# A selective scan and a spectral filter: the input load, the root of the group norms and the loads of B and C at other slots

## The chip, the core and the metric

The kernel runs on one core of a Trainium2 chip. A core has five engines with an instruction queue each: PE (TensorE, matrix products and transposes), DVE (VectorE), ACT (ScalarE), POOL (GpSimd) and SP (SyncE, which here only issues DMAs). Each queue runs in program order; engines wait for one another, and for DMAs, by semaphores. The metric is the time of one execution on the device in microseconds (us), the median of several runs. A profile is one further execution, recorded by the hardware.

## The reference

The input x is (4, 128, 128, 128): batch, channel, height, width. Two layers follow.

Layer 0 is a selective scan over the 16,384 pixels of an image, channels 128, inner width 256, 16 states:

```
xm  = relu(x @ w1 + b1) @ w2 + b2
u,z = split(xm @ in_proj);   u = silu(causal_conv4(u))
dt,B,C = split(u @ x_proj)            # 8, 16 and 16 columns
delta  = softplus(dt @ dt_proj + b)
h = h * exp(delta * A) + delta * B * u      # per inner channel and state
y = (sum over states of h * C + u * D) * silu(z)
out = silu(group_norm(y @ out_proj, 4 groups)) + x
```

Layer 1 aggregates its input (group norm, a 128 by 128 product, relu, mean over the image, softmax over 4 weights), and filters each image in the frequency domain: forward transform, product with a mix of four complex filters and with the transform itself, backward transform, plus half of the input.

## The kernel before

**Tiling.** `block0` does layer 0 and the aggregation, `block1` the spectral filter. In `block0` an image is cut into 32 chunks of T = 512 pixels, so there are 128 chunks for four images. The 256 inner channels are 2 halves (j) of 128; each half is 4 groups (r) of 32 channels, and 32 channels with 4 states fill the 128 partitions. One such tile of 128 x 512 is scanned by one DVE instruction, `nc.vector.tensor_tensor_scan` (L405). A chunk has 2 x 4 x 4 = 32 of them, two a slot, so a chunk has NP = 16 slots.

**Order.** Nothing is scheduled by a tool: each piece of work is entered as (slot, phase, function) in `todo`, and L493 to L497 emit them slot by slot, in a slot by phase: turn, sums, pe, exps, late, act, pool, dbu, gate, scans, dve, end. The slots in `pre(k)` (L313) are relative to the chunk before k: slot 16 is the first slot in which chunk k is scanned. Negative slots lie in the chunk before that. So each engine, SP too, works on chunks k and k+1 interleaved. What this order does to one engine's queue is all that decides what may run when.

**The preparation of chunk k** (`pre`): `load` brings the chunk's input xt (one buffer) by SP; `h1_mm`, `h1_act`, `xm_mm`, `xm_act` are the first two products; `cv_mm`, `silu_act` make u; `xd_mm`, `xd_act` make dt, B and C as xd (40 x 512) and store B and C into a DRAM tile bc; `dt_mm`, `dt_act` make delta, and SP stores it into a DRAM tile dd, half by half; `du_pool` (L303, POOL) makes du = delta * u and SP stores it into dd too. The DRAM tiles are there to be read back spread over partitions:

- `bc_load` (L253): B as rB (four DMAs of 192 KB) and C as rC (four of 256 KB), each row copied to 32 partitions;
- `rep_load(j)` (L311): for half j, delta as rdelta and du as rdu (four DMAs of 256 KB each), each row copied to the 4 states of its channel. Half 0 is issued at slot 9, half 1 at slot 16. Both tiles have two buffers.

`du_turn` (PE) and `bt_act` (ACT) make the product delta * B * u for the first of every four tiles in another way, by way of transposes.

**The scan of a chunk.** ACT makes da = exp(delta * A) (`exps`, L387), POOL makes hb = rdu * rB for the other three of every four tiles (`dbu`, L354, at every even slot, two slots ahead of its scans), DVE scans (L405), then h is multiplied by rC, by DVE for two of four tiles (L407) and by POOL for the other two (`scans`, L412). PE sums over states (`sums`, L426). The first `dbu` of chunk k is emitted at slot 14 of the chunk before: it is the first instruction that reads rB of k and rdu of half 0 of k.

**SP's queue** in chunk k-1, in order: rep_load(1) of k-1 (slot 0), the store of bc (slot 4), the store of an output, bc_load (slot 5), two stores of delta (slot 6), xt of the next chunk (slot 7), two stores of du (slot 7, phase pool), rep_load(0) (slot 9). A DMA whose semaphore is not there holds up all that stand behind it.

**Norms.** `finish` applies the group norm of a finished image, its silu and the residual, while the next image is scanned; it reads the parts of x and of the output back (xr, of) in slots 13 and 14, in chunks 2 to 17 of the next image (48 chunks in all, called norm chunks below; the others are called plain), and then aggregates. `group_norm` (L500) is run twice an image: statistics on DVE, two small products with ACT work between them, then `root_act` (L529, a square root on ACT) and `invert` (L532, a reciprocal on DVE), and last what needs the result (`then`: three small ACT instructions, or the scaled weights of the aggregation, followed by `bias_mm` on PE and `bias_act` on ACT). The norms of the last image lie in `block1`, whose slots are thirds of a unit of eight channels of an image.

Of the kernel before, what the change touches and what calls it, by code (L numbers as in the profile page):

```python
# [146 lines left out]
def block0(tc, s):  # L147
# [4 lines left out]
    with ExitStack() as ctx:  # L152
# [22 lines left out]
        def pre(k):  # L175
# [130 lines left out]
            def rep_load(j):  # L306
# [4 lines left out]
                        nc.sync.dma_start(out=t[m * DG : (m + 1) * DG], in_=rows)  # L311

            return [  # L313
                (-9, "pe", load), (-7, "pe", h1_mm), (-6, "act", h1_act), (-5, "pe", xm_mm), (-4, "act", xm_act),
                (0, "pe", partial(cv_mm, 0)), (1, "pe", partial(cv_mm, 1)), (2, "act", silu_act),
                (NP - 3, "pe", z_mm), (NP - 1, "act", z_act), (NP + 2, "act", z_silu), (3, "pe", xd_mm), (4, "act", xd_act), (5, "pe", dt_mm), (5, "pe", xd_turn),
                (5, "act", bc_load), (6, "act", dt_act), (7, "act", xd_turn_act), (7, "pool", partial(du_pool, 0)),
                (7, "pool", partial(du_pool, 1)), (8, "pe", partial(du_turn, 0)), (9, "act", partial(rep_load, 0)),
                (8, "pool", partial(bt_act, 0, 0, 1)), (9, "act", partial(bt_act, 0, 1, 5)),
                (10, "act", partial(bt_act, 0, 5, 8)), (11, "pe", partial(du_turn, 1)),  # L320
                (11, "pool", partial(bt_act, 1, 0, 1)), (12, "act", partial(bt_act, 1, 1, 2)),
# [139 lines left out]
        todo = defaultdict(list)  # L461
        for k in range(n_chunks):
            for at, phase, f in pre(k) + post(k):
                todo[at + (k - 1) * NP, phase].append(f)
# [16 lines left out]
        for b in range(B - 1):  # L481
            for at, phase, f in finish(s, io, b, NP + 7, norm, agg):
                todo[at + (b + 1) * NCH * NP, phase].append(f)
# [16 lines left out]
def group_norm(s, io, b, mat, which, stat, at, then):  # L500


    nc = s.nc
    g = {}

    def small(n, m=1):
        g[n] = io.small.tile([P, m], F32, tag=n, name=f"{n}_{which}_{b}")
        return g[n]

    def aggregate():  # L510
        nc.vector.bn_aggr(small("mv", 2), stat().rearrange("p n q -> p (n q)"))

    def mean_mm():
        ps = g["ps"] = io.psum(f"gm_{which}_{b}")
        nc.tensor.matmul(ps[:, 0:1], getattr(s, mat), g["mv"][:, 0:1], start=True, stop=True)

    def spread_act():
        mv = g["mv"]
        nc.scalar.copy(small("mean"), g["ps"][:, 0:1])
        q = small("q")  # L520
        nc.scalar.activation(q, mv[:, 0:1], AF.Square, scale=-1.0, bias=g["mean"])
        nc.scalar.activation(q, q, AF.Identity, bias=mv[:, 1:2])

    def var_mm():
        ps = g["ps"] = io.psum(f"gv_{which}_{b}")
        nc.tensor.matmul(ps[:, 0:1], getattr(s, mat), g["q"], start=True, stop=True)

    def root_act():
        nc.scalar.activation(small("rstd"), g["ps"][:, 0:1], AF.Sqrt, bias=s.eps)  # L529

    def invert():
        nc.vector.reciprocal(g["rstd"], g["rstd"])  # L532
        then(g["mean"], g["rstd"])

    return [
        (at, "dve", aggregate), (at, "end", mean_mm), (at + 1, "act", spread_act), (at + 3, "pe", var_mm),
        (at + 3, "act", root_act), (at + 3, "dve", invert),
    ]


def finish(s, io, b, first, norm, agg, add="dve"):
# [87 lines left out]
    def weights_act():  # L629
        nc.scalar.activation(s.wts[b], g["lg"], AF.Identity, scale=g["total"])  # L630

    todo = group_norm(s, io, b, "g0", 0, lambda: stats[b], first, start)
    for i in range(NCH):
        at = norm(i)
# [3 lines left out]
        ]  # L638
    c = at[2] + 5
    todo += group_norm(s, io, b, "g1", 1, lambda: g["stat"], c, middle)  # L640
    todo += [(c + 4, "pe", bias_mm), (c + 4, "act", bias_act)]
    for i in range(NCH):
        at = agg(i)
        todo += [
# [3 lines left out]
    c = at[2] + 1  # L648
# [6 lines left out]
def block1(tc, s):  # L655
# [10 lines left out]
    with ExitStack() as ctx:  # L666
# [35 lines left out]
        t1 = norm(NCH - 1)[2] + 14  # L702
        todo = defaultdict(list)
        steps = finish(s, io, B - 1, 0, norm, lambda i: (t1 + i - 3, t1 + i, t1 + i, None), "add")
        for at, phase, f in steps:
            todo[at, phase].append(f)
# [269 lines left out]
```

## Time and profile before

| What | Value |
|---|---|
| median of 3 runs | 7330.66 us (7328.43 to 7332.73) |
| the profiled execution's own time | 7341.55 us |
| its span | 7339.5 us |
| DVE, POOL, ACT, PE busy | 96%, 94%, 83%, 80% of the span |
| DMA queue of SP | 1240.28 MB, 69.2% of the 16 engines' time |
| scan part, filter part | up to about 6510 us, from then on |

The page gives each engine's busy time and what its idle time waited for; a line such as L405 is a line of the kernel's source. Tiles go by the program's names: `hb<-rdu,rB` writes hb from rdu and rB. SPq is SP's queue of DMA issues. The profiler misses some records, so counts of a few per cent too few are no sign of missing work. In the list of windows, the columns are the stretch and its length, the busy time of PE, of weight loads, of DVE, ACT and POOL with counts, the granted PE clock, the DMA share and GB/s.

### The profile page before, as it was taken

Reading aid. Unit: us, or ns where it says so; the run is one execution under the profiler, and the core shown is the slowest. Engines: PE = TensorE matmul, PEld = TensorE weight load, DVE = VectorE, ACT = ScalarE, POOL = GpSimd, SP = SyncE. Lnnn points to the kernel's source line nnn. Section 1 sums busy time; section 2 is a strip of 40 time slices with the busy share of each in tenths; the row PEclk is TensorE's granted clock in tenths of the full one; section 3 lists DMA queues with packets and bytes.
Section 4 is the critical chain, followed back from the end, with each engine's and each line's share of the span. In section 5 each row is a group of like instructions: output and inputs, shape, how many; then the busy total and the mean of one; then the engine's idle time right before and its main releaser. Section 6 shows DMA issues by size and latency. Waiting matters only on the chain.

```text
span 7339.5 us, 90375 instructions
## 1 busy us (share of the span) xinstructions
PE 5890.0 (80%) x25908; PEld 2648.4 (36%) x25908; DVE 7022.4 (96%) x8168; ACT 6064.9 (83%) x13183; POOL 6896.1 (94%) x3188
## 2 busy tenths in 40 slices
PE   7877877877777788887777788887777788868999
PEld 2322322332222233332222233332222233348999
DVE  7999999999999999999999999999999999978777
ACT  6888888888888888888888888888888888867886
POOL 6999999999999999999999999999999999977787
PEclk8888888888888889898899888888999888889999
DMA  5766666666777767667777676677777766758666
GB/s 139 163 156 148 157 156 155 150 159 165 187 181 176 182 159 166 169 163 178 180 177 188 165 172 167 158 171 173 178 187 173 178 165 156 175 142 255 187 165 169
DMA packets 864134, 1246.32 MB, mean 170 GB/s; under 512 B 78856, under 2 KB 318608, under 8 KB 863632
## 3 DMA queue, kind: packets, MB, share of 16 engines
q1 hardware_dynamic: 863488, 1240.28, 69.2%
q8 instruction: 204, 3.34, 0.2%
q14 instruction: 298, 2.44, 0.1%
q10 hardware_dynamic: 144, 0.26, 0.0%
HBM read 996.97 MB, written 243.27 MB: 169 GB/s over the span
## 4 chain that ended last, share of the span: by engine, by line
DVE 16%; ACT 14%; DMA 14%; PE 12%; issue 5%; POOL 2%; SPq 1%; DVEq 0%; ACTq 0%; POOLq 0%
DVE da L405 7%; ACT da L387 6%; DVE h L405 4%; DMA rdelta<-dd 3%; DMA xt<-in_x 3%; DVE hb L407 2%; PE pp_h L190 2%; DMA of<-ob 2%; ACT bt L295 1%; DMA dd<-delta 1%; DMA rB<-bc 1%; PE pa L780 1%; DMA xr<-in_x 1%; ACT L387 1%; PE y L426 1%
## 5 line engine op out<-in xcount | busy, mean ns | idle before, releaser
L354 POOL TENSOR_TENSOR hb<-rdu,rB 128x1536 f32<-128x1536 f32 (+2 forms) x1536 | 3603.3, 2362 | 38.6 <-DMA rdu<-dd 35.3
L387 ACT ACTIVATE da<-rdelta,amat 128x512 f32<-128x512 f32 x4096 | 2677.1, 694 | 63.2 <-DVE h L405 60.0
L412 POOL TENSOR_TENSOR hb<-h,rC 128x1024 f32<-128x1024 f32 (+1 forms) x1072 | 2433.5, 2272 | 179.2 <-DVE h L405 162.5
L405 DVE TENSOR_TENSOR_SCAN da<-da,st,hb 128x512 f32<-128x512 f32 x1976 | 2425.0, 1272 | 11.7 <-POOL hb L354 5.3
L426 PE MATMUL y<-hb,sel 128*32 128x512 f32 x8192 | 1313.3, 717 | 3.1 <-POOL hb L412 2.7
L407 DVE TENSOR_TENSOR hb<-da,rC 128x512 f32<-128x512 f32 x2040 | 1301.3, 679 | 3.0
L405 DVE TENSOR_TENSOR_SCAN h<-da,st,b 128x512 f32<-128x512 f32 x992 | 1264.1, 1274 | 23.6 <-ACT da L387 7.0
L405 DVE TENSOR_TENSOR_SCAN h<-da,st,hb 128x512 f32<-128x512 f32 x1000 | 1256.8, 1261 | 2.0 <-ACT da L387 1.6
L374 PE MATMUL b<-ident,bt 128*128 128x128 f32 x4096 | 759.9, 309 | 613.3 <-DVE h L405 499.0
L225 PE MATMUL pp_cv<-xm,wck 128*128 128x512 f32 x2048 | 1018.7, 642 | 32.9 <-ACT zs L219 32.0
L374 PEld LDWEIGHTS b<-ident,bt 128*128 128x128 f32 x4096 | 548.7, 157 | 1187.2 <-DVE h L405 788.2
L295 ACT ACTIVATE bt<-pt_dut,xdt 128x256 f32<-128x256 f32 x2048 | 838.2, 471 | 132.4 <-PE pt_dut L284 132.3
L408 ACT COPY st<-da 128x1 f32<-128x1 f32 x2040 | 282.5, 161 | 767.9 <-DVE hb L407 765.8
L225 PEld LDWEIGHTS pp_cv<-xm,wck 128*128 128x128 f32 x2048 | 399.3, 206 | 700.2 <-issue 461.9
L190 PE MATMUL pp_h<-xt,w 128*128 128x512 f32 x512 | 387.3, 899 | 262.5 <-DMA xt<-in_x 208.3
L759 POOL TENSOR_TENSOR wb<-wb,term 128x1040 f32<-128x1040 f32 x192 | 461.0, 2401 | 90.0 <-ACT term L753 75.3
L284 PE MATMUL pt_dut<-ident,du 128*128 128x128 f32 x1024 | 209.3, 326 | 279.8 <-ACT st L408 270.3
L422 PE MATMUL y<-u,diag 128*128 128x512 f32 x512 | 297.8, 665 | 146.8 <-DVE zs L436 146.5
L303 POOL TENSOR_TENSOR du<-delta,u 128x512 f32<-128x512 f32 x256 | 319.1, 1268 | 27.2 <-ACT delta L266 27.2
L387 ACT ACT_TABLE_LOAD x262 | 336.1, 1283 | 4.7
L284 PEld LDWEIGHTS pt_dut<-ident,du 128*128 128x128 f32 x1024 | 126.9, 156 | 574.4 <-POOL du L303 436.2
L190 PEld LDWEIGHTS pp_h<-xt,w 128*128 128x128 f32 x512 | 124.6, 269 | 547.2 <-DMA xt<-in_x 261.1
(138 smaller groups left out, 8084.0 us busy)
## 6 DMA issues: line engine op xcount, KB each, us to landing
rdelta<-dd SPq DMA_DIRECT2D x1024, 256.0 KB, 4.8
rdu<-dd SPq DMA_DIRECT2D x1024, 256.0 KB, 7.8
rC<-bc SPq DMA_DIRECT2D x512, 256.0 KB, 7.5
rB<-bc SPq DMA_DIRECT2D x512, 192.0 KB, 4.8
dd<-delta SPq DMA_DIRECT2D x256, 256.0 KB, 7.3
dd<-du SPq DMA_DIRECT2D x256, 256.0 KB, 6.4
ft<-in_filt_w SPq DMA_DIRECT2D x104, 520.0 KB, 7.0
ob<-o SPq DMA_DIRECT2D x128, 256.0 KB, 2.1
```

The lines of the kernel that those rows point to most:

```text
L190: nc.tensor.matmul(ps["h", j], s.w1[:, j * P : (j + 1) * P], d["xt"], start=True, stop=True)
L225: nc.tensor.matmul(ps["cv", j], w, d["xm"][:, t : t + T], start=t == 0, stop=t == KC - 1)
L284: nc.tensor.transpose(ps["dut"][:, 2 * t + j, :], d["du"][:, j, at : at + P], s.ident)
L295: nc.scalar.activation(d["bt"][:, 2 * h + t, :, q, :], src, AF.Copy, scale=d["xdt"][:, 2 * h + t, R + q : R + q + 1])
L354: nc.gpsimd.tensor_tensor(hb[:, p : p + n, :], d["du", j][:, m : m + n, :], d["B"][:, p - 1 : p - 1 + n, :], ALU.mult)
L374: nc.tensor.transpose(b[:, t * P : (t + 1) * P], src, s.ident)
L387: nc.scalar.activation(d["da", p][q], d["delta", j][:, m, :], AF.Exp, scale=s.amat[:, c : c + 1])
L405: nc.vector.tensor_tensor_scan(o, das[q], b, init, ALU.mult, ALU.add)
L407: nc.vector.tensor_tensor(hb[:, p + q, :], das[q], d["C"][:, p + q, :], ALU.mult)
L412: nc.gpsimd.tensor_tensor(hb[:, ps, :], h[:, q, :], d["C"][:, ps, :], ALU.mult)
L426: nc.tensor.matmul(y[m * DG : (m + 1) * DG, :], s.sel, d["hb", j, r][:, p, :], start=False, stop=r == NG - 1)
L759: nc.gpsimd.tensor_tensor(wb, wb, u[n].terms[f], ALU.add)
```

## The change

Three things move; no instruction is added or removed.

- xt of chunk k is loaded at slot -14 instead of -9, both in phase pe. In terms of the chunk before, that is slot 2 instead of 7 of the one in which it is used at slot 9.
- `bc_load` goes from slot 5, phase act, to slot 7, phase dve. On SP it then stands behind the two stores of delta and the two of du, and directly ahead of `rep_load(0)`.
- In `group_norm` the root goes from slot at + 3 to at + 5, the reciprocal (with `then`) from at + 3 to at + 6. `bias_mm` and `bias_act` go from c + 4 to c + 7 and c + 8.

```diff
             return [
-                (-9, "pe", load), (-7, "pe", h1_mm), (-6, "act", h1_act), (-5, "pe", xm_mm), (-4, "act", xm_act),
+                (-14, "pe", load), (-7, "pe", h1_mm), (-6, "act", h1_act), (-5, "pe", xm_mm), (-4, "act", xm_act),
                 (0, "pe", partial(cv_mm, 0)), (1, "pe", partial(cv_mm, 1)), (2, "act", silu_act),
...
-                (5, "act", bc_load), (6, "act", dt_act), (7, "act", xd_turn_act), (7, "pool", partial(du_pool, 0)),
-                (7, "pool", partial(du_pool, 1)), (8, "pe", partial(du_turn, 0)), (9, "act", partial(rep_load, 0)),
+                (6, "act", dt_act), (7, "act", xd_turn_act), (7, "pool", partial(du_pool, 0)),
+                (7, "pool", partial(du_pool, 1)), (7, "dve", bc_load), (8, "pe", partial(du_turn, 0)), (9, "act", partial(rep_load, 0)),
...
         (at, "dve", aggregate), (at, "end", mean_mm), (at + 1, "act", spread_act), (at + 3, "pe", var_mm),
-        (at + 3, "act", root_act), (at + 3, "dve", invert),
+        (at + 5, "act", root_act), (at + 6, "dve", invert),
...
     todo += group_norm(s, io, b, "g1", 1, lambda: g["stat"], c, middle)
-    todo += [(c + 4, "pe", bias_mm), (c + 4, "act", bias_act)]
+    todo += [(c + 7, "pe", bias_mm), (c + 8, "act", bias_act)]
```

## The prediction

> **What bounds the kernel now.** I read the page's busy shares first, then the waits of VectorE and GpSimd between 100 and 6520 us (the scan part; the filter part follows), then the order of time of SyncE and GpSimd over one chunk, then the DMA share in short windows.
>
> ```profile
> PE 5890.0 (80%) x25908; PEld 2648.4 (36%) x25908; DVE 7022.4 (96%) x8168; ACT 6064.9 (83%) x13183; POOL 6896.1 (94%) x3188
> ```
>
> The waits of VectorE (engine, instruction, releaser; total us, times, longest), then single rows of GpSimd's and PE's lists:
>
> ```profile
> DVE rstd L532 <- ACT rstd L529: 12.0, 6, 2.6
> DVE h L405 <- ACT da L387: 9.7, 23, 1.8
> DVE da L405 <- ACT da L387: 5.8, 14, 0.9
> ```
> ```profile
> POOL hb L354 <- DMA rdu<-dd: 14.3, 17, 2.6
> ```
> ```profile
> PE pp_h L190 <- DMA xt<-in_x: 208.3, 111, 8.8
> ```
>
> VectorE is the bound of the scan part: all its waits there are 35 us (the three shown, and 7.8 more, of which 5.6 for hb). That is the ceiling of any gain. But GpSimd stands right behind it: a 49.95 us chunk holds about 48.5 us of its work, a chunk with norm work (51.13 us) about 50.1. A delay on GpSimd of more than about 1 us in every chunk can't be absorbed. And its wait for rdu, 14.3 us in 17 waits, says that those copies land only just in time already.
>
> The waits of scans on da and hb come mostly from the late input. At one such place (PE, ACT, DVE in order of time):
>
> ```profile
> 1286.69 3.78 PE L190 MATMUL pp_h<-xt,w 128*128 128x512 f32 x4 [3.00 <-DMA xt<-in_x]
> ...
> 1294.01 0.47 ACT L295 ACTIVATE bt<-pt_dut,xdt 128x256 f32<-128x256 f32 x1 [1.50 <-PE pt_dut L284]
> ...
> 1295.34 2.47 DVE L405 TENSOR_TENSOR_SCAN da<-da,st,hb 128x512 f32<-128x512 f32 x2 [1.04 <-POOL hb L354]
> ```
>
> xt is late, the turn of du queues behind it on PE, bt waits on ACT, the exponentials behind bt are late, then the scans. Added by hand, VectorE's gaps at slots 12 and 13 are some 17 us over the run.
>
> Now SyncE's queue over a chunk, then GpSimd's:
>
> ```profile
> 1322.58 1.82 SPq L253 DMA_DIRECT2D rB<-bc  x4
> 1324.51 1.78 SPq L253 DMA_DIRECT2D rC<-bc  x4
> 1327.18 0.92 SPq L268 DMA_DIRECT2D dd<-delta  x2
> 1328.19 0.75 SPq L185 DMA_DIRECT2D xt<-in_x  x1
> 1329.81 1.77 SPq L304 DMA_DIRECT2D dd<-du  x2
> 1335.26 1.74 SPq L311 DMA_DIRECT2D rdelta<-dd  x4
> 1337.17 1.73 SPq L311 DMA_DIRECT2D rdu<-dd  x4
> ```
> ```profile
> 1328.51 2.50 POOL L303 TENSOR_TENSOR du<-delta,u 128x512 f32<-128x512 f32 x2
> 1330.96 3.45 POOL L354 TENSOR_TENSOR hb<-rdu,rB 128x1536 f32<-128x1536 f32 x1
> ...
> 1347.64 3.44 POOL L354 TENSOR_TENSOR hb<-rdu,rB 128x1536 f32<-128x1536 f32 x1 [0.26 <-DMA rdu<-dd]
> ```
>
> du of the next chunk ends at 1331.01. The first product that needs its copies, call it u0, starts at 1347.64, 16.6 us later, after a wait of 0.26 us for the last rdu. Between them GpSimd worked without a break. B and C, 1.8 MB, were sent ahead of all this, from 1322.58 on.
>
> ```profile
> 1326.00:1338.00 12.00, 6.84 (x26) 2.58 (x19) 11.86 (x13) 11.53 (x27) 11.86 (x8) 0.50 0.96 252
> ...
> 1351.00:1364.00 13.00, 10.66 (x41) 4.24 (x41) 13.00 (x15) 9.07 (x20) 12.57 (x7) 1.00 0.78 162
> ```
>
> The last two numbers are the DMA share and GB/s. From about 1324 to 1347 the 16 engines are full: B, C, the stores, xt and the copies form one burst that uses time before du exists. The second row is a lone burst, the eight copies of the second half (2.1 MB, issued from 1350.36 on): 162 GB/s at share 0.78, so 208 GB/s when full.
>
> **What the Trainium skill says.** "DMA: Bandwidth & Descriptors", section "Issuing engines are not separate DMA queues", has every DMA run on the same 16 engines; the trace agrees (full windows, one queue with 69.2% of the engines' time), so what is sent late delays what follows it. Its section "Anatomy of one DMA" gives some 2 us fixed per DMA: the lone burst takes 12.0 us from first issue to last landing, of which 2.1 MB at 208 GB/s are 10.1; 1.9 is left, which agrees. "GPSIMD Engine Reference", section 3.1, has a two-input add of 2048 fp32 at 4497 ns on GpSimd, 2.2 ns an element; here 1024 take 2.36 us, 2.3 ns an element. So GpSimd won't run faster to catch up.
>
> **The change, part by part.**
>
> *xt five slots sooner.* One DMA of 256 KB moves from behind the delta stores to slot 2, into the idle stretch after the copies of the second half. Its buffer is free since slot 9 of the chunk before. On SyncE it passes B and C, the bc store and the delta stores; it waits for nothing that is late. It takes away the 208.3 us of PE waits, and by that the 17 us of VectorE: −17 at most, if VectorE stays the bound.
>
> *Root and reciprocal later.* The eight reciprocals wait 17.1 us for the root: 12.0 for six in the scan part, 5.1 for two in the filter part; with about 1 us of follow-on gaps, −13 at most in the scan part. Nothing reads the result before bias_mm, moved too, and the first norm step five slots on. No instruction is added. In the filter part PE is full (197.6 of 200 us at 6800 to 7000), so I count 2 of the 5.1.
>
> *B and C behind the stores.* Eight DMA issues leave the place before delta and stand behind both du stores, ahead of the first copies of delta and du. In the built program SyncE's order is delta, delta, du, du, B×4, C×4, rdelta×4, rdu×4. SyncE waits at the du stores for GpSimd, as before, but now B and C queue behind that wait. So 1.8 MB that ran before du was ready now starts after du, in front of the 2.1 MB that u0 needs. (Each DMA of SyncE also waits for the landing of the eighth before it; with seven still queued the engines stay full, so that costs nothing.) The wait from du's end to u0's start is now:
> - second du store issued, and the first B behind it: 0.45 us (store 0.32, and the sequencer's step)
> - first B issued to last C landed: 11.7 us, the median of this trace's bursts of B and C (here 1322.58 to 1335.1)
> - eight copies behind them at 1.22 us each, the spacing of their landings: 9.8 us
> - GpSimd sees the last landing: 0.2 us
>
> Together 22.15 us. From bytes alone it is 3.93 MB / 208 GB/s = 18.9, plus 1.9, 0.45 and 0.2: 21.4. I take 22.1.
>
> u0 can't start before that. From u0's start to the next du's end GpSimd has 31.5 us of back-to-back work: 11 groups of rows from 1347.64 to the next du's end at 1380.96, 33.3 us less 1.8 of waits for VectorE and small gaps. The loop du → copies → u0 → next du is closed in program order, so its period is 31.5 + 22.1 = 53.6 us, in every chunk. Before, the loop was 31.5 + 16.4 and GpSimd's work filled 16.4 to 18.7 of it.
>
> du's end runs from 80.1 to 6448.0 us over 126 such periods: 6367.9 us. After: 126 × 53.6 = 6753.6. That is +386. In this loop VectorE has 4 us to spare per chunk (2.5 with norm work), so the 17 and 13 us above vanish into that and are worth nothing. Queued behind u0 on GpSimd are the C products of the last slots and all later hb; VectorE's second scan of slot 0 waits for u0's end (3.45 us after the landing) and everything after it on VectorE. Late next: the turn of du on PE and bt on ACT at slot 8, about when VectorE is at slot 9; 0 to 0.6 us per chunk, inside the slack.
>
> The first chunk: the wait for rdu ends about 1 us later. Sum: +386 + 1 − 2 = +385. The profiled execution took 7341.55 us (span 7339.5); the runs' median is 7330.66, 11 us less. On the median: 7716.
>
> **The rivals.**
> 1. *The copies still come in time (faster).* Place: the last rdu landing against u0. If du-to-u0 stays under 18.1 us (the plain chunk's mean of 49.6, less 31.5), the loop doesn't bind, and xt and root pay: −17 −13 −2, near 7299. It needs 3.93 MB in 15.5 us (18.1 less 1.9, 0.45 and 0.2), 253 GB/s, against 208 measured for the lone burst; for it speaks only that the mixed window at 1326 reached 252, with stores and xt in it. Improbable.
> 2. *A shorter loop.* B and C run faster with no bc store and o store ahead of them, and the path is 20.6: period 52.1, 126 × 52.1 = 6565, +197: 7528.
> 3. *A longer loop.* The late du holds ACT and through it VectorE beyond its slack, most in norm chunks, or xr and of loads mix in: period 54.8, +537: 7868.
> 4. *No difference*: only if VectorE's gains and a small overrun cancel, around a path of 18.5.
>
> **How the numbers follow.** The loop at 52.7 to 54.3 (7600 to 7805): 0.75. Shorter (7350 to 7600): 0.08. Longer: 0.10. In time, faster: 0.05. No difference: 0.02. The runs before spread by 0.06%; 0.2% is about what can be told. The range 7560 to 7845 takes the forecast case and the near halves of the shorter and longer ones. Slower 0.93, same 0.02, faster 0.05.
>
> **What would show it.** Right: GpSimd's wait for rdu goes from 14 to some 550 us (78 × 5.1 + 48 × 3.4) with about 127 waits; VectorE waits for hb of L354 about 400 us, once a chunk at slot 0; du ends come 53.6 us apart in plain and in norm chunks alike; PE's wait for xt and the wait of rstd nearly go; VectorE's share falls to about 91%. Wrong: du ends 49 to 51 us apart, or norm chunks longer than plain ones, or GpSimd waiting on VectorE instead.

## The result, and the profile after

The changed kernel takes 7773.0 us, median of 6 runs (7765.21 to 7775.01), against 7335.4 for the kernel before, measured beside it (7328.43 to 7344.72). The ratio is 1.0591, 95% interval 1.0581 to 1.0602: 5.9% slower. Forecast were 7716 us and a range of 7560 to 7845. The profiled execution took 7765.21 us, its span is 7763.4, 423.9 us longer than that of before.

The busy shares of the page:

```profile
PE 6051.4 (78%) x25908; PEld 2695.9 (35%) x25908; DVE 7044.9 (91%) x8168; ACT 6054.8 (78%) x13183; POOL 6881.0 (89%) x3188
```

VectorE and GpSimd work as long as before, to within 25 us, in a span 424 us longer. No engine is full any more, and the DMA queue takes 67.4% of its engines' time. So the added time is waiting. Whose it is, the lists of waits between 100 and 6950 us say, VectorE's first:

```profile
DVE h L405 <- POOL hb L354: 402.9, 130, 4.9
DVE h L405 <- ACT da L387: 17.6, 30, 1.5
```
```profile
POOL hb L354 <- DMA rdelta<-dd: 272.4, 49, 7.3
POOL hb L354 <- issue: 124.5, 23, 7.4
POOL hb L354 <- DMA xr<-in_x: 78.6, 18, 7.1
POOL hb L354 <- DMA of<-ob: 71.0, 18, 5.3
POOL hb L354 <- DMA rdu<-dd: 54.8, 13, 6.2
POOL hb L354 <- DMA x<-x: 25.9, 5, 5.8
```

The six rows of GpSimd are one wait under six names. The instruction waits for the four rB and the four rdu at once; an eighth of the landings of SyncE's DMAs (593 of 4744) has no record, and others fall close by, so the wait is put down to a neighbour. Together they are 627.3 us in 126 waits, one a chunk, where before this instruction had 14.3 us in 17 waits for rdu and 17.1 in 24 under all names. VectorE's wait for what GpSimd then makes is 402.9 us. Its waits for the root are gone from the list, and PE's 208.3 us for xt too.

SyncE's and GpSimd's rows of one chunk, to be held against those of the prediction:

```profile
1312.42 0.90 SPq L268 DMA_DIRECT2D dd<-delta  x2
1316.87 1.55 SPq L304 DMA_DIRECT2D dd<-du  x2
1318.52 1.80 SPq L253 DMA_DIRECT2D rB<-bc  x4
1320.42 1.80 SPq L253 DMA_DIRECT2D rC<-bc  x4
1322.33 3.55 SPq L311 DMA_DIRECT2D rdelta<-dd  x4
1326.74 3.94 SPq L311 DMA_DIRECT2D rdu<-dd  x4
```
```profile
1315.55 2.52 POOL L303 TENSOR_TENSOR du<-delta,u 128x512 f32<-128x512 f32 x2
1318.00 3.49 POOL L354 TENSOR_TENSOR hb<-rdu,rB 128x1536 f32<-128x1536 f32 x1
...
1340.70 3.43 POOL L354 TENSOR_TENSOR hb<-rdu,rB 128x1536 f32<-128x1536 f32 x1 [6.24 <-DMA rdelta<-dd]
...
1369.53 2.48 POOL L303 TENSOR_TENSOR du<-delta,u 128x512 f32<-128x512 f32 x2
```

du ends at 1318.07 and the first B is issued 0.45 us later; before, it was 8.4 us earlier than du's end. u0 starts 22.6 us after du's end and has waited 6.24 us. The next du ends 53.94 us after this one. The list of windows (DMA share and GB/s last) shows the full burst and the idle stretch that came in its place:

```profile
1321.00:1340.00 19.00, 15.15 (x59) 5.34 (x56) 18.97 (x22) 16.73 (x44) 13.45 (x8) 0.86 1.04 214
...
1350.00:1370.00 20.00, 13.92 (x57) 4.50 (x55) 19.86 (x22) 18.37 (x34) 20.00 (x10) 0.84 0.12 43
```

For 19 us the 16 DMA engines are full and GpSimd, with 13.45 us of work, stands idle for the rest; from 1350 on GpSimd is full for 20 us and the DMA engines are at 0.12. (In the 10 us left out the copies of the second half run.) The two take turns, which is what a loop looks like. The Trainium skill, "Perfetto Trace Analysis", section "Identifying the Most-Contended Engine", looks for the bottleneck by occupancy; here that would name VectorE at 91%, which is not what sets the time. The wait that is repeated once a chunk is.

### The profile page after: what moved, and what is told of

Its sections match the earlier page's. It is cut to its first block, busy times and chain, and to the rows that moved or that the text cites. A ratio compares the mean times of both kernels' runs of the same rounds, so it can differ in the third digit from the quotient of the medians.

```text
span 7763.4 us, 89854 instructions
## 1 busy us (share of the span) xinstructions
PE 6051.4 (78%) x25908; PEld 2695.9 (35%) x25908; DVE 7044.9 (91%) x8168; ACT 6054.8 (78%) x13183; POOL 6881.0 (89%) x3188
## 3 DMA queue, kind: packets, MB, share of 16 engines
q1 hardware_dynamic: 863488, 1240.28, 67.4%
## 4 chain that ended last, share of the span: by engine, by line
POOL 47%; DMA 23%; PE 10%; ACT 6%; issue 5%; DVE 5%; SPq 3%; POOLq 0%; DVEq 0%; ACTq 0%
POOL hb L354 25%; POOL hb L412 18%; DMA rdelta<-dd 8%; DMA rC<-bc 5%; POOL du L303 4%; DMA rdu<-dd 3%; ACT da L387 2%; SPq L253 2%; DMA xr<-in_x 2%; DVE da L405 2%; DMA rB<-bc 2%; DMA of<-ob 2%; PE pa L780 1%; PE y L426 1%; PE px L794 1%
## 5 line engine op out<-in xcount | busy, mean ns | idle before, releaser
L412 POOL TENSOR_TENSOR hb<-h,rC 128x1024 f32<-128x1024 f32 (+1 forms) x1072 | 2425.9, 2265 | 11.7 <-DVE h L405 11.6
L426 PE MATMUL y<-hb,sel 128*32 128x512 f32 x8192 | 1381.8, 752 | 380.3 <-POOL hb L412 378.5
L225 PE MATMUL pp_cv<-xm,wck 128*128 128x512 f32 x2048 | 1172.4, 724 | 41.7 <-ACT zs L219 40.6
L225 PEld LDWEIGHTS pp_cv<-xm,wck 128*128 128x128 f32 x2048 | 460.4, 237 | 853.4 <-issue 652.6
L284 PE MATMUL pt_dut<-ident,du 128*128 128x128 f32 x1024 | 245.0, 351 | 491.3 <-POOL du L303 333.7
L426 PEld LDWEIGHTS y<-hb,sel 128*32 128x32 f32 x8192 | 175.3, 117 | 750.8 <-POOL hb L412 448.0
L422 PE MATMUL y<-u,diag 128*128 128x512 f32 x512 | 275.9, 621 | 81.8 <-DVE zs L436 81.6
L190 PE MATMUL pp_h<-xt,w 128*128 128x512 f32 x512 | 319.6, 754 | 8.1 <-DMA w<-in_mlp_w1T 4.4
```

What stands on the lines that cost most here:

```text
L225: nc.tensor.matmul(ps["cv", j], w, d["xm"][:, t : t + T], start=t == 0, stop=t == KC - 1)
L284: nc.tensor.transpose(ps["dut"][:, 2 * t + j, :], d["du"][:, j, at : at + P], s.ident)
L412: nc.gpsimd.tensor_tensor(hb[:, ps, :], h[:, q, :], d["C"][:, ps, :], ALU.mult)
L426: nc.tensor.matmul(y[m * DG : (m + 1) * DG, :], s.sel, d["hb", j, r][:, p, :], start=False, stop=r == NG - 1)
```

## The experiments

Two numbers were taken from the instruction records of every run, over the plain chunks (norm chunks in brackets): the way from du's end to u0's start, and the period from one du's end to the next. Medians in us:

| Kernel | du to u0 | period | period less du to u0 | ratio to before (95% interval) |
|---|---|---|---|---|
| before | 17.40 (18.63) | 49.95 (51.13) | 32.5 (32.5) | 1 |
| the change | 22.50 (22.52) | 53.84 (53.86) | 31.3 (31.3) | 1.0591 (1.0581 to 1.0602) |
| B and C alone | 22.50 (22.49) | 53.83 (53.90) | 31.3 (31.4) | 1.0596 (1.0581 to 1.0610) |
| B and C put back | 17.39 (18.63) | 49.81 (51.13) | 32.4 (32.5) | 0.9964 (0.9952 to 0.9977) |
| B and C behind the copies | 17.40 (18.64) | 49.93 (51.13) | 32.5 (32.5) | 0.9973 (0.9962 to 0.9984) |
| B and C ahead of du's stores | 18.22 (19.85) | 49.59 (51.28) | 31.4 (31.4) | 0.9985 (0.9978 to 0.9992) |
| C alone behind | 18.83 (18.89) | 50.21 (51.13) | 31.4 (32.2) | 1.0026 (1.0017 to 1.0035) |
| one load more ahead | 23.89 (23.89) | 55.20 (55.22) | 31.3 (31.3) | 1.0807 (1.0792 to 1.0821) |
| the same from dd | 23.84 (23.88) | 55.16 (55.20) | 31.3 (31.3) | 1.0814 (1.0796 to 1.0832) |
| one load more behind | 22.63 (22.66) | 53.95 (54.00) | 31.3 (31.3) | 1.0601 (1.0585 to 1.0617) |
| xt alone | 17.38 (18.63) | 49.82 (51.13) | 32.4 (32.5) | 0.9967 (0.9954 to 0.9979) |
| norms alone | 17.39 (18.63) | 49.94 (51.13) | 32.6 (32.5) | 0.9988 (0.9981 to 0.9994) |

The fourth column shows where GpSimd waits. At 31.3 to 31.4 us it works from u0 to the next du without a gap, so that its only wait is at u0, for the copies. Where the rest is longer, it waits for VectorE in between. This alone doesn't say that the loop sets the time: B and C ahead of du's stores also have 31.4 and are no slower than before, for there the copies come late for another reason than du (more on this below).

The plain periods near 49.9 are no fine measure: VectorE has one product more in every second chunk, and in the kernel before plain chunks alternate between 49.95 and 49.21, 49.6 in the mean. The median falls on the one or the other.

**Which of the three edits.** B and C alone, and the two others without them:

```diff
# B and C alone, against before
-                (5, "act", bc_load), (6, "act", dt_act), ...
+                (6, "act", dt_act), ... (7, "pool", partial(du_pool, 1)), (7, "dve", bc_load), ...
# B and C put back, against the change
-                (6, "act", dt_act), ... (7, "dve", bc_load), ...
+                (5, "act", bc_load), (6, "act", dt_act), ...
```

> Only the loads of B and C move (slot 7, phase dve, behind the stores of du); xt and the norms stay where they were before. Loop theory (du on GpSimd, then B and C, then the copies, then the first product): the whole loss is here, period 53.9 us a chunk, about 7773 us (7755 to 7795). Rival, that the earlier xt or the later root share in the loss: clearly below 7750. If B and C alone cost nothing: 7335.

> The change with the loads of B and C put back to slot 5; xt early and the root late stay. Loop theory: the loop is 31.5 + 16.4 us again and does not bind, VectorE's gaps at slots 12 and 13 (17 us) and its waits for the root (13 us) are gone: about 7305 us (7295 to 7320), and the period of a plain chunk is 49.6 us. Rival, that xt or the root cost something of their own: above 7335.

Measured: 7778.49 us and 7314.22 us, beside 7343.52 for before. The whole loss is with B and C. The other two edits together gain 0.36%, 29 us on the medians. With B and C put back, VectorE's list for 100 to 6520 us no longer has the root (12.0 us before), and of its two rows on da (5.8 and 9.7 us before) this is left:

```profile
DVE da L405 <- ACT da L387: 5.3, 8, 0.9
...
DVE h L405 <- ACT da L387: 2.4, 5, 0.8
```

The two edits were also run one at a time:

```diff
# xt alone, against before
-                (-9, "pe", load), ...
+                (-14, "pe", load), ...
# norms alone, against before
-        (at + 3, "act", root_act), (at + 3, "dve", invert),
+        (at + 5, "act", root_act), (at + 6, "dve", invert),
-    todo += [(c + 4, "pe", bias_mm), (c + 4, "act", bias_act)]
+    todo += [(c + 7, "pe", bias_mm), (c + 8, "act", bias_act)]
```

> Only xt moves, to slot 2. It should take away the late products behind xt and with them VectorE's gaps at slots 12 and 13, some 17 us: a ratio of 0.9977 to the kernel before. If the early load is worth nothing on its own: 1.000.

> Only the root, the reciprocal and the bias of the norms move. It should take away VectorE's six waits for the root in the scan part (12 us) and a little behind them: a ratio of 0.9982. If those waits only move elsewhere: 1.000.

Measured: 7322.09 and 7336.99 us, beside 7344.95 for before. Each is worth something on its own: xt 0.33% (about 24 us, where 17 were expected), the norms 0.12% (about 9, where 13 were expected). Each interval includes what was expected. Their sum, 0.45%, isn't told apart from the 0.36% of both together.

**Late, or in front of the copies.** B and C were sent later still, to behind the copies of delta and du:

```diff
-                (7, "pool", partial(du_pool, 1)), (7, "dve", bc_load), ...
+                (7, "pool", partial(du_pool, 1)), (9, "dve", bc_load), ...
```

> The change with B and C still later: behind the first copies of delta and du (slot 9, phase dve). They are then later than in the change, but no longer ahead of what the first product needs. Loop theory: from the end of du the copies take about 0.45 + 2.1 + 9.8 us, then the four loads of B 3.5, so the product starts some 16 to 17.5 us after du, the loop is under 49.6 us and does not bind: 7300 to 7340. Rival, that B and C must simply be early (their own lateness costs): 7773 or more.

Measured: 7323.53 us. Being late costs B and C almost nothing; it is standing in front of the copies that costs. The last rdu now lands 12.7 us after du's end instead of 22.1, and u0 starts 17.4 us after du as before, when GpSimd comes to it. GpSimd waits for B or C in 21 places, 16.6 us in all.

**Ahead of the stores of du, still behind those of delta.** This moves the burst by two store issues only:

```diff
-                (6, "act", dt_act), (7, "act", xd_turn_act), ... (7, "dve", bc_load), ...
+                (6, "act", dt_act), (6, "act", bc_load), (7, "act", xd_turn_act), ...
```

> The change with B and C between the stores of delta and those of du (slot 6, phase act, after dt_act), some 3 us sooner. Loop theory: the burst of 11.8 us starts 2.9 us before du ends, the stores of du and the eight copies follow: the first product starts about 20.3 us after du, period 51.7 us: +2.1 in 78 plain chunks, +0.6 in 48 norm chunks, about 7530 us (7480 to 7590). Rival, that only the place behind the stores of delta counts: 7773. Rival, that any place ahead of du is early enough: 7305.

Measured: 7331.11 us, a ratio of 0.9985. All three expectations miss it: the loop theory's 7530 is far off, and so is 7773; 7305 is nearest. SyncE's and GpSimd's rows of one chunk show why:

```profile
1321.67 0.90 SPq L268 DMA_DIRECT2D dd<-delta  x2
1322.66 1.85 SPq L253 DMA_DIRECT2D rB<-bc  x4
1324.61 1.79 SPq L253 DMA_DIRECT2D rC<-bc  x4
1326.99 1.55 SPq L304 DMA_DIRECT2D dd<-du  x2
```
```profile
1325.69 2.49 POOL L303 TENSOR_TENSOR du<-delta,u 128x512 f32<-128x512 f32 x2
...
1345.22 3.44 POOL L354 TENSOR_TENSOR hb<-rdu,rB 128x1536 f32<-128x1536 f32 x1 [0.67 <-DMA rdu<-dd]
```

I had taken the way from du to u0 as fixed, with the first B 2.9 us ahead of du's end. But B and C now wait only for the stores of delta, and delta is made by ACT, not by GpSimd. When GpSimd falls behind, B and C don't: the first B goes out 5.5 us ahead of du's end here, 4.5 in the median of the plain chunks and 3.2 in that of the norm chunks. The delay is paid once and then the burst stays ahead of du: u0 of the third chunk waits 5.3 us, and for the next chunk the first B goes out 5.7 us ahead of du's end instead of 2.8, and the way is 17.4 us instead of 21.7. u0 still waits for its copies in nearly every chunk (170.6 us in 125 waits), but it now follows the first B at a steady distance, 22.7 us with a standard deviation of 0.3 in the plain chunks, while its distance from du varies by 0.6. So the copies come at a time that du doesn't set, and VectorE is hardly held up (the time is 17 us above that of B and C put back):

```profile
DVE h L405 <- POOL hb L354: 9.6, 16, 1.1
```

In the change, B and C wait behind GpSimd's own du in SyncE's queue, so every delay of GpSimd is passed on to them and comes back to it. Two stores' place in a queue, on the other side of a wait, decides over 440 us.

**How much in front.** C alone was left behind du's stores, B put back:

```diff
-            def bc_load():
+            def bc_load(only):
                 for q, tag in enumerate("BC"):
+                    if tag != only:
+                        continue
...
+                (5, "act", partial(bc_load, "B")), (6, "act", dt_act), ...
-                ... (7, "dve", bc_load), ...
+                ... (7, "dve", partial(bc_load, "C")), ...
```

> The change with only C behind the stores of du; B goes back to slot 5. Loop theory: from the end of du 0.44, four loads of C in 6.7, eight copies in 9.8 and 0.4 to the product make 17.4 us; with 31.4 of GpSimd's work the loop is 48.8 us, under the 49.6 that VectorE takes, so nothing binds: a ratio of 0.996 to 1.000, though the same stores of du stand ahead of C. Rival, that any load behind the wait for du costs its own time every chunk: half of the loss stays, 1.02 to 1.03.

Measured: 7363.44 us, 0.26% above before: a little outside the loop theory's range, and far from the rival's. The four loads of C take longer than I had taken, 8.4 us from the first issue to the last landing instead of 6.7 (the first lands 2.82 us after the last store of du has landed, the others follow at 1.23). So du to u0 is 18.83 us and the loop 50.21, just above VectorE's 49.6 in the plain chunks, and not binding in the norm chunks (51.13). That is the edge of the loop, hit by accident. Against B and C put back (7314.22 us), which has the other two edits too, it is 49 us, and 78 plain chunks that are 0.6 us longer make 47. 768 KB less in front take 3.6 us off the period of the change, and the period is again the way plus 31.4.

Then one load more, a copy of the chunk's x into a spare tile that nothing reads: ahead of the copies, from two sources, and behind them.

```diff
# ahead of the copies, at the end of bc_load
+                spare = p1.tile([P, T], F32, tag="spare", name=f"spare_{k}")
+                nc.sync.dma_start(out=spare, in_=s.xflat[b, :, i * T : (i + 1) * T])
# the same, from dd
+                nc.sync.dma_start(out=spare, in_=d["dd"][0, 0:P, :])
# behind them: the first two lines at the end of rep_load, if j == 0
```

> The whole change, and behind the loads of C one more load of 256 KB that nobody reads (the rows of x again, into a spare tile), ahead of the copies. Loop theory: the burst between du and the first product grows by the spacing of such a load, 0.65 us, and the period with it, 53.9 to 54.5 us: 126 times 0.65 = +82 us on the time of the change, a ratio of 1.070 to the kernel before (1.067 to 1.074). Rival, that the wait is one of SyncE's order or of a fixed latency and not of the bytes in front: 1.059.

> The whole change with the same extra load of 256 KB, but behind the eight copies instead of ahead of them. The bytes and the number of DMAs are those of the run with it ahead. Loop theory: nothing that the first product waits for stands behind it, the loop stays 53.9 us: a ratio of 1.059 (1.056 to 1.063). Rival, that more DMA work as such, wherever it stands, costs the 1.4 us a chunk: 1.081.

> The whole change with an extra load of 256 KB ahead of the copies again, but from the tile dd, whose rows lie one after the other in memory, where x has its rows 64 KB apart. If the rows' distance made the first extra load cost 1.4 us instead of 0.65: the loop is 54.5 us, a ratio of 1.070. If it is the place among loads that spread rows (1.2 us apart): 1.081 again.

Measured: 7938.81 and 7941.31 us ahead, 7785.19 behind. SyncE's rows with the load ahead (behind the new lines, the line numbers are two higher):

```profile
1356.14 1.80 SPq L253 DMA_DIRECT2D rC<-bc  x4
1358.46 0.35 SPq L255 DMA_DIRECT2D spare<-in_x  x1
1359.23 3.36 SPq L313 DMA_DIRECT2D rdelta<-dd  x4
```

The same DMA behind the copies leaves the ratio at 1.0601, ahead of them it makes 1.0807. So it isn't DMA work as such, it's what lies between du and u0. The way and the period both grow by 1.3 to 1.4 us, and 126 × 1.36 are 171 us, against 166 measured to the change (7938.81 less 7773.0; 158 by the two ratios). The landings show where it goes: from the last C to the first rdelta it is 2.43 us in the median instead of 1.26, and the burst of B and C ahead of it takes 12.0 instead of 11.8. The size was not the 0.65 us that I had expected, but twice that. I had taken it from the landings of stores and of xt, which come 0.6 apart, and had put the load among loads that come 1.2 apart. The rows' distance in memory isn't it: from dd, where rows follow one another, it costs the same.

## Why the prediction was right

*The bound and the loop.* Right in mechanism, place and size. It said that GpSimd stands close behind VectorE, and that the copies land just in time; that B and C behind du's stores close a loop through du, B, C, copies and u0; that plain and norm chunks would take the same time (53.84 and 53.86); that GpSimd would wait some 550 us for rdu in about 127 waits (627 in 126) and VectorE about 400 us for hb (402.9), once a chunk at slot 0; that VectorE would fall to about 91%.

*The terms of the loop.* From du's end to the first B 0.45 us (measured 0.44), to the last C 11.7 (11.8), to the last rdu 9.8 (9.8): right. That GpSimd sees the last landing: 0.2 us, measured 0.3. The whole way is 22.5 instead of 22.1. GpSimd's work from u0 to du: 31.5, measured 31.3; the two misses are of opposite sign, and that they partly cancel is luck. (Medians of parts don't add up exactly.) So 53.6 became, as a mean, 53.9 in the plain and 53.95 in the norm chunks, against 52.1 and 54.8 of the shorter and the longer loop. From the second du to the last it makes 6792.4 us instead of 6753.6: that +39 is all that the span misses (+423.9 instead of +385). What lies ahead of the second du and behind the last changed by −2.4 and +1.7, where +1 and −2 were forecast. On the medians, 437.6, some 14 us more are within what single executions differ by (16 us before, 10 after).

*The first chunk.* Wrong by little: its first product was to come 1 us later. It came 2.4 us sooner (48.8 us instead of 51.1), and so did the end of the second du.

*xt and the root.* That they vanish into VectorE's slack is right: B and C alone cost as much as the whole change. Their worth without the loop, −17 and −13, was about right (24 and 9 measured).

*The rivals.* That the copies come in time would have needed 253 GB/s; the burst ran at 214. The slack of the threshold, 18.1 us from du to u0, was put right too: at 18.83 the loop just binds.

*What I had wrong until the runs.* Not in the prediction but in the expectations: that the way from du to u0 shrinks only by as much as B and C go out sooner. B and C ahead of du's stores cost next to nothing, for the burst then hangs on delta and is out of the loop.

The version that beats both kernels is the change with B and C put back: 7314.22 us, 0.9964 of before. xt alone, with 0.9967, isn't told apart from it.

## What to carry to other kernels

Where an engine's own result goes out by DMA and comes back to it, look for the loop: its work from the return to the next sending, plus everything that queues between sending and return. If that sum is over the pace of the busiest engine, it is the period, however idle every engine looks. A load that is moved behind a wait in a queue is not just later, it joins the loop of whatever that wait waits for; if it doesn't need that result, keep it ahead of the wait, or behind the transfer that the loop needs.

## What was not expected of the hardware

A load of 256 KB that nobody reads, put among loads that spread rows over partitions, cost 1.3 to 1.4 us a chunk, where plain loads and stores of 256 KB among themselves land 0.6 to 0.7 us apart (in the kernel before xt lands 0.59 behind the second store of delta, and the first store of du 0.67 behind xt). "DMA: Bandwidth & Descriptors", section "Latency and other measured facts", has copies slow down where rows lie 2 MB and more apart (164 GB/s, 207 at 512 KB); x's rows are 64 KB apart, and a source without gaps cost the same, so distance is no part of it here. Two loads that were there all along show the same: xr and of land 0.65 us apart in the kernel before, and 1.15 in the change, where the copies of the second half follow them directly (in the kernel before those land 3 us later).

The trace also has every packet that a DMA engine moved. One of 2 KB took 84 to 87 ns in the median where only plain loads and stores ran, and about 160 among the spreading loads, in the stretches of the extra load too. A load of 256 KB is 128 such packets, 8 for each of the 16 DMA engines, which makes 0.7 us or 1.3 us (an estimate from these figures, with the packets evenly spread). So the extra load costs what its packets take in that place. Why a packet takes twice as long there stays open.
